# Stores of the first pair begun on GpSimd, and k times v with its weights' factors on VectorE, in a linear-attention block gated by a Hadamard feed-forward

## The chip, the cores and the metric

The kernel runs on one core of one Trainium2 chip. A core has TensorE (PE, matrix products, with weight loads listed as PEld), VectorE (DVE), ScalarE (ACT), GpSimd (POOL) and SyncE (SP), each with a queue of instructions that it takes in order, and DMA engines that move data between DRAM and the on-chip memory. The metric is the device time of one execution in microseconds (us), lower is better.

## The reference

The input x is 8 x 512 x 512 in fp32 (batch, length L, width D). Everything is computed in fp32.

```python
xn = layernorm(x)
# s: linear attention, 16 heads of 32
q, k, v = (xn @ W.T + b for each of Wq, Wk, Wv)
phi_q, phi_k = elu(q) + 1, elu(k) + 1
kv = cumsum(phi_k * v, axis=length)         # elementwise, no products between channels
s = ((phi_q * kv) * 32**-0.5) @ Wo.T + bo
# g: feed-forward, inner width 2048, Hadamard transforms (fwht) around the weights
h = fwht(xn * SU_ug)
u = silu((h @ W_gate.T) * scale_gate) * ((h @ W_up.T) * scale_up)
g = silu((fwht(u * SU_dp) @ W_down.T) * scale_dp)
return x + s * g
```

## The kernel before, in words

**Products in seven.** Every large matrix product is done in 2 x 2 blocks with seven products in place of eight (P1, P2, P7, P3, P4, P5, P6 are the seven places). For that, each weight and each set of tokens is first turned into seven factors: four blocks are loaded, and three more plus a new P7 are made by four additions (`encode_weights`, L305 to L308; `encode_tokens`, L297 to L300). On the gate and up weights this is done twice, one level inside the other, from the point where the second level exists ("gu" weights, L630).

**Pairs.** The batch is taken in 4 pairs p = 0..3 of two elements. A pair goes through: layernorm and transposes; attention in two groups g of channels (k, v, q in turn; then elu plus one, the product k times v, the cumulative sums along the length as scans, and q times the sums, `co`, with its factors); then 4 units u of the inner width. A unit makes the gate (`gate`, silu on ACT), the up part (`up`, gate times up is `ho`, with its factors), and after units 1 and 3 half of the down projection (`down`). `project_out` (output projection, `pz_o`, `px_o`) stands in unit 0.

**The first pair is different.** It reads the raw weights. For gate, up and down the Hadamard transform is put into the weights: butterflies on VectorE (L930 to L933 for gate and up, L969 and L974 for down), a product with a small Hadamard matrix on TensorE (`pw_gate`, `pwd`), a scale on ACT (L945, and in `fold_down`). The factors are made once and stored in DRAM for the later pairs, which only stream them: `keep_w` (L319) stores the factors of k, v, q, o; `inner_w` (L391 to L414) makes the outer factors of gate and up from the weights `w0` and `w1` in a three-slot tile `s_gate` or `s_up` (L408) and stores each factor as it is made (L400, into `d_gu`); `down_w` (L388) and `first_half_down` (L1018) store those of down (`d_down`), from `wd_f`, which `fold_down` (L997) stores. In `inner_w`, P5 goes to slot 0, P6 to slot 1, P3 to slot 2, and P7 to slot 0 again, so that P7 waits until the store of P5 has read its slot. All these stores, 73 in number, are begun on SP, which also begins nearly all loads. Units 0 to 2 of the first pair use `gate` and `up`; unit 3, and all units of later pairs, use `hidden_unit` with the streamed weights.

**What sets the order.** The program is traced in the order of an agenda: `at(place, fn)` puts a step so many places ahead, and `advance` runs through them; a group of seven products with two steps each is 14 places. Work for VectorE that is not urgent is put in the lists `later` (with `soon=True`: the urgent one) and handed out by `pace` behind each sum of an output (L468, the sum of a copied PSUM bank and another bank). `get_w` asks for weights three ahead, so that their loads, folds and factors (the `steps`) are spread over the groups before. `background` gives traced work a lower priority. A scheduler then fixes one queue per engine. Buffers come from pools (4 weight tiles, 6 tiles `t8` of 8 KB a partition, 6 snapshots, one `xin` tile for x or the s tiles, PSUM banks px 3, py 1, pz 2, t 2), so that a load can wait for the last reader of the tile that was there.

**What the change touches.** `keep_w`, `down_w`, `inner_w`, `fold_down`, `first_half_down` (the stores); `inner_w` (the last factor); `with_v` (L716, k times v on GpSimd, two operations of 128 x 1024) and `sums` (L722, four scans of 128 x 512 on VectorE); `up` (L793 to L798, ho and its factors on GpSimd, one of the products on VectorE); `first_w` (the factors of k, v, q and o on GpSimd). Other steps named later: L180, the layernorm scale of the first x; L271 to L284, the transposes and the tokens' factors `xo`; L333, factors of `wd` for the second half of down; L350 and L367, loads of raw gate weights and of `wd`; L528, products of o and down; L661, a sum of the two-level products; L777, silu of the gate; L831 and L835, sums of 128 x 1024 on GpSimd in `hidden_unit`.

Of the kernel before, what the change touches and what calls it, by code (L numbers as in the profile page):

```python
# [10 lines left out]
ALU = mybir.AluOpType  # L11
# [6 lines left out]
P1, P2, P7, P3, P4, P5, P6 = range(7)  # L18
# [3 lines left out]
def kernel(  # L22
# [27 lines left out]
    nc = tc.nc  # L50
    P = 128
    B, L, D = x.shape
# [5 lines left out]
    NU = NG // 2  # L58
# [27 lines left out]
    def later(us, fn, *args, soon=False):  # L86
        (urgent if soon else idle).append((us, fn, args))
# [16 lines left out]
    at = 0  # L104
# [13 lines left out]
    ones = const.tile([P, 1], F32, tag="ones", name="ones")  # L118
# [197 lines left out]

    def keep_w(name, w):
        d = dram.tile([P, 2 * 7 * P], F32, tag=f"d_{name}", name=f"d_{name}")
        nc.sync.dma_start(d, w.rearrange("p j s e -> p (j s e)"))  # L319
        kept[name] = d  # L320
        return w

# [51 lines left out]
    def down_w(u, j):  # L374

        t = t8.tile([P, 2, 7, P], F32, tag="t", name=f"wd_{u}_{j}")
        w = by_factor(t)
        rows_w(w, wd_f, u + NU * j, NG)

        def encode():  # L380
            for o, a, b, op in (
                (P5, P7, P4, ALU.add), (P6, P5, P1, ALU.subtract), (P3, P2, P6, ALU.subtract), (P7, P1, P7, ALU.subtract)
            ):
                later(0.5, nc.vector.tensor_tensor, w[:, o], w[:, a], w[:, b], op)
            later(0.0, store)

        def store():
            nc.sync.dma_start(wd[u // 2][:, :, 2 * (u % 2) + j], w)  # L388
            wd_made[u // 2] += 1

        at(8, encode)  # L391

    def inner_w(m, u, w0, w1):

        if u not in inner:
            inner[u] = dram.tile([P, 7, 2, 7, P], F32, tag=f"d_gu_{u}", name=f"d_gu_{u}")
        d = inner[u][:, :, ("gate", "up").index(m)]

        def store(c, t):
            nc.sync.dma_start(d[:, :, c, :], t)  # L400

        store(P1, w0[:, 0])
        store(P2, w0[:, 1])
        store(P4, w1[:, 1])
        t = xin.tile([P, 3, 7, P], F32, tag="x", name=f"s_{m}_{u}")

        def made(c, i, a, b, op):
            nc.vector.tensor_tensor(t[:, i], a, b, op)  # L408
            store(c, t[:, i])

        later(1.0, made, P5, 0, w1[:, 0], w1[:, 1], ALU.add, soon=True)
        later(1.0, made, P6, 1, t[:, 0], w0[:, 0], ALU.subtract, soon=True)
        later(1.0, made, P3, 2, w0[:, 1], t[:, 1], ALU.subtract, soon=True)
        later(1.0, made, P7, 0, w0[:, 0], w1[:, 0], ALU.subtract, soon=True)  # L414

# [4 lines left out]
    def at(place, fn):  # L422
        agenda.append((now[0] + place, now[1], fn))
        now[1] += 1
# [259 lines left out]
    def attention(p, xo, co, get_w):  # L684
        def project(m, g, then):
            w = get_w(m, g)
            r = t8.tile([P, 2, 2, L], F32, tag="t", name=f"{m}_{p}_{g}")
            b = (col("b" + m, g), col("b" + m, g + 2))

            def whole(px):  # L690
                nc.scalar.activation(r[:, 0, 1], px, AF.Identity, bias=b[0])  # L691
                then(r)

            group(
                f"{m}_{p}_{g}", [w[:, 0], w[:, 1]], x_rhs(xo),
                (r[:, 0, 0], r[:, 1, 0], r[:, 1, 1]), whole, b,
            )

        def elu_plus_one(r, name):
            neg = t8.tile([P, 2, 2, L], F32, tag="t", name=f"neg_{name}")  # L700
            for h in range(2):
                nc.scalar.activation(neg[:, h], r[:, h], AF.Relu, scale=-1.0)
                nc.scalar.activation(neg[:, h], neg[:, h], AF.Exp, scale=-1.0)
                nc.vector.scalar_tensor_tensor(r[:, h], r[:, h], 1.0, neg[:, h], ALU.add, ALU.max)

        def heads(g):
            phi = {}

            def with_k(k):
                phi["k"] = k  # L710
                elu_plus_one(k, f"k_{p}_{g}")

            def with_v(v):
                k = phi["k"]
                for h in range(2):
                    nc.gpsimd.tensor_tensor(v[:, h], v[:, h], k[:, h], ALU.mult)  # L716
                at(4, lambda: sums(k, v))

            def sums(k, v):
                for h in range(2):  # L720
                    for s in range(2):
                        nc.vector.tensor_tensor_scan(  # L722
                            k[:, h, s], ones.to_broadcast([P, L]), v[:, h, s], 0.0, ALU.mult, ALU.add
                        )

            def with_q(q):
                k = phi["k"]
                elu_plus_one(q, f"q_{p}_{g}")
                for h in range(2):
                    nc.vector.scalar_tensor_tensor(  # L730
                        co[:, g, h : h + 3 : 2, :], k[:, h], QSCALE, q[:, h], ALU.mult, ALU.mult
                    )
                encode_tokens(nc.gpsimd, co[:, g])

            project("k", g, with_k)
            project("v", g, with_v)
            project("q", g, with_q)

        for g in range(2):
            heads(g)  # L740
# [43 lines left out]
        )  # L784
        return g

    def up(p, f, g, xo, ho, get_w):

        w = get_w("up", f)
        r = t8.tile([P, 2, 2, L], F32, tag="t", name=f"u_{p}_{f}")  # L790

        def with_up(px):
            nc.gpsimd.tensor_tensor(ho[:, P1], g[:, 0, 0], r[:, 0, 0], ALU.mult)  # L793
            nc.vector.tensor_tensor(ho[:, P7], g[:, 0, 1], px, ALU.mult)
            nc.gpsimd.tensor_tensor(ho[:, P2 : P3 + 1 : 2], g[:, 1], r[:, 1], ALU.mult)
            encode_tokens(nc.gpsimd, ho)

        group(  # L798
            f"up_{p}_{f}", [w[:, 0], w[:, 1]], x_rhs(xo),
            (r[:, 0, 0], r[:, 1, 0], r[:, 1, 1]), with_up,  # L800
        )
# [181 lines left out]
    def fold_down(o):  # L983
        r = rs[:, o % 2]
        for a in range(NF // 4):
            p = ps.tile([P, 4, P], F32, tag="t", name=f"pwd_{o}_{a}")
            tc.keep_in_program_order(
                nc.tensor.matmul(
                    p.rearrange("p c e -> p (c e)"), had,
                    r[:, 4 * a : 4 * a + 4].rearrange("p c e -> p (c e)"), start=True, stop=True,  # L990
                )
            )
            for c in range(4):
                nc.scalar.activation(
                    r[:, 4 * a + c], p[:, c], AF.Copy, scale=su_dp[:, 4 * a + c : 4 * a + c + 1]
                )
        nc.sync.dma_start(wd_f[:, o * P : (o + 1) * P].rearrange("(c p) e -> p c e", p=P), r)  # L997

    def first_half_down():

        n = 4 * 2 * P
        w = [rd[:, i * n : (i + 1) * n] for i in range(7)]
        for a in range(2):
            for b in range(2):
                t = w[(P1, P2, P7, P4)[2 * a + b]].rearrange("p (u j e) -> u p j e", u=2, j=2)
                d = wd_f[:, a * 2 * P : (a + 1) * 2 * P].rearrange("(b j u p) e -> b u p j e", b=2, j=2, p=P)
                for u in range(2):
                    nc.sync.dma_start(t[u], d[b, u])

        def factors():  # L1010
            for i, x, y, op in (
                (P5, P7, P4, ALU.add), (P6, P5, P1, ALU.subtract), (P3, P2, P6, ALU.subtract), (P7, P1, P7, ALU.subtract)
            ):
                later(1.2, nc.vector.tensor_tensor, w[i], w[x], w[y], op, soon=True)
            later(0.0, at, 4, store, soon=True)

        def store():
            nc.sync.dma_start(wd[0].rearrange("p i k e -> p (i k e)"), rd)  # L1018
            wd_made[0] = 4

        at(8, factors)
# [4 lines left out]
    def first_w(m, g):  # L1026


        if m == "gate":
            return folded_w(m, wgate_t, g)  # L1030
        if m == "up":
            return folded_w(m, wup_t, g)
        name, eng = f"{m}_{g}", nc.gpsimd
        if m == "o":
            t = new_w(name)
            w = by_factor(t)
            rows_w(w, wo_t, g, 2)
        else:
            t = w = raw_w(name, sources[m], 0, 2, 1, g * P, 2 * P)

        def encode():
            encode_weights(eng, w)
            keep_w(name, t)

        return w, [(5, encode)]
# [131 lines left out]
    for p in range(B // 2):  # L1177
# [11 lines left out]
        for u in range(NU):  # L1189
            if p == 0 and u < NU - 1:  # L1190
# [3 lines left out]
                    project_out(p, co, get_w)  # L1194
                ho = hop.tile([P, 2, 7, L], F32, tag="h", name=f"ho_{p}_{u}")
                for m in range(2):
                    up(p, u + m * NU, gs[m], xo, ho[:, m], get_w)
            else:
                if p == 0:
                    catch_up()  # L1200
# [78 lines left out]
```

## Time and profile before

| | before |
|---|---|
| median of 3 runs | 1566.42 us (1566.15 to 1566.45) |
| the profiled execution | 1564.62 us |
| its span on the core | 1562.8 us (1.8 us lie around it) |
| mean granted TensorE clock | 0.993 |
| busy: PE, PEld, DVE, ACT, POOL | 98%, 72%, 63%, 27%, 32% |
| instructions: PE, DVE, ACT, POOL | 5924, 1379, 664, 280 |
| DMA queue q1 (hardware, from SP) | 272.27 MB, 53.3% of 16 engines |

The profile is one execution. A row of a group or a timeline names the line of the kernel, the engine, the operation and "out<-in" by the program's names. "idle before <-" tells how long an engine stood before the instruction and what it waited for. `pz_q`, `px_gate` and the like are PSUM banks, named for the bank and the stage. A matmul in fp32 of the program shows as two rows of the trace.

### The profile page before, as it was taken

To read this page: it belongs to the slowest core of one execution; us is meant where nothing else is said; L and a number is where in the kernel's file an instruction comes from. 1 tells how busy PE (TensorE), PEld (TensorE's weight loads), DVE (VectorE), ACT (ScalarE), POOL (GpSimd) and SP (SyncE) were. 2 spreads that over 40 slices of the span, in tenths; PEclk is the share of its full clock that TensorE was granted. 3 is DMA by queue.
4 is the path that set the end of the run, shared out by engine and by line. 5 is a ranking of instruction groups with operands and counts; after the bars stand their busy time and mean duration, and the time that the engine had idled before them with its cause. 6 is when DMAs were issued, how large, how long until landed. Compare 5 with 4: busy or idle time off the path is not lost.

```text
span 1562.8 us, 15732 instructions
## 1 busy us (share of the span) xinstructions
PE 1529.4 (98%) x5924; PEld 1127.0 (72%) x5924; DVE 985.1 (63%) x1379; ACT 418.8 (27%) x664; POOL 497.5 (32%) x280
## 2 busy tenths in 40 slices
PE   7999999998999999999999999999999999999998
PEld 3335545845884588888885488888886468888887
DVE  5897785677866674716676574725675476543673
ACT  4443341142114521112215431111212431111211
POOL 4633144004321262304612235301622236110731
PEclk9999999999999999999999999999999999999999
DMA  8244867797785344344575434336474233535462
GB/s 280 78 153 152 268 218 225 232 275 270 200 304 196 91 158 155 108 152 165 157 286 213 102 137 148 135 102 195 153 249 171 85 106 117 185 99 177 155 260 85
DMA packets 197693, 273.31 MB, mean 175 GB/s; under 512 B 56817, under 2 KB 155121, under 8 KB 193393
## 3 DMA queue, kind: packets, MB, share of 16 engines
q1 hardware_dynamic: 197472, 272.27, 53.3%
q8 instruction: 47, 0.77, 0.2%
q14 instruction: 30, 0.24, 0.0%
q10 hardware_dynamic: 144, 0.03, 0.0%
HBM read 196.25 MB, written 76.02 MB: 174 GB/s over the span
## 4 chain that ended last, share of the span: by engine, by line
PE 88%; DVE 4%; DMA 3%; issue 2%; POOL 1%; ACT 1%; SPq 1%; POOLq 0%; DVEq 0%; ACTq 0%
PE px_gu L630 20%; PE px_dn L528 13%; PE pz_gu L630 10%; PE pz_dn L528 6%; PE py_gu L630 5%; PE py_dn L528 4%; PE px_k L452 3%; PE px_v L452 3%; PE px_o L528 3%; PE px_q L452 3%; PE pz_o L528 2%; PE pz_k L452 2%; PE px_gate L452 2%; PE pz_q L452 2%; PE pz_v L452 1%
## 5 line engine op out<-in xcount | busy, mean ns | idle before, releaser
L630 PE MATMUL px_gu<-xo,w_gu 128*128 128x256 f32 x1456 | 348.9, 381 | 0.0
L630 PEld LDWEIGHTS px_gu<-xo,w_gu 128*128 128x128 f32 x1456 | 277.5, 191 | 44.2 <-issue 5.0
L528 PE MATMUL px_dn<-w_down,ho 128*128 128x256 f32 x1024 | 228.9, 379 | 0.0
L528 PEld LDWEIGHTS px_dn<-w_down,ho 128*128 128x128 f32 x1024 | 194.9, 190 | 28.7 <-issue 2.9
L630 PE MATMUL pz_gu<-xo,w_gu 128*128 128x256 f32 x728 | 188.6, 382 | 5.4 <-DVE a L661 5.2
L831 POOL TENSOR_TENSOR u<-u,v 128x1024 f32<-128x1024 f32 x26 | 60.8, 2363 | 371.2 <-DVE u L668 347.5
L630 PEld LDWEIGHTS pz_gu<-xo,w_gu 128*128 128x128 f32 x728 | 138.3, 191 | 26.2 <-DVE a L661 6.1
L528 PE MATMUL pz_dn<-w_down,ho 128*128 128x256 f32 x496 | 112.4, 380 | 3.2 <-DVE u L468 3.2
L528 PEld LDWEIGHTS pz_dn<-w_down,ho 128*128 128x128 f32 x496 | 93.9, 190 | 17.0 <-DVE u L468 3.6
L630 PE MATMUL py_gu<-xo,w_gu 128*128 128x256 f32 x364 | 93.5, 379 | 0.0
L876 POOL TENSOR_TENSOR s<-s,d 128x512 f32<-128x512 f32 x30 | 40.0, 1333 | 165.5 <-ACT d L875 126.4
L716 POOL TENSOR_TENSOR v<-v,k 128x1024 f32<-128x1024 f32 x16 | 43.0, 2685 | 138.9 <-ACT v L691 111.2
L630 PEld LDWEIGHTS py_gu<-xo,w_gu 128*128 128x128 f32 x364 | 69.3, 190 | 9.3
L835 POOL TENSOR_TENSOR v<-v,r 128x1024 f32<-128x1024 f32 x26 | 60.9, 2362 | 27.7 <-DVE r L668 27.7
L793 POOL TENSOR_TENSOR ho<-g,u 128x512 f32<-128x512 f32 x6 | 10.9, 1812 | 161.0 <-DVE u L468 151.1
L452 PE MATMUL px_k<-xo,w_k 128*128 128x512 f32 x128 | 61.6, 603 | 0.0
L452 PE MATMUL px_v<-xo,w_v 128*128 128x512 f32 x128 | 60.8, 595 | 0.0
L821 ACT ACTIVATE a<-a,cols_sb 128x512 f32<-128x512 f32 x26 | 18.8, 722 | 155.2 <-DVE a L668 153.4
L452 PE MATMUL px_q<-xo,w_q 128*128 128x512 f32 x128 | 60.2, 593 | 0.0
L722 DVE TENSOR_TENSOR_SCAN k<-ones,v 128x512 f32<-128x512 f32 x32 | 40.9, 1317 | 28.6 <-POOL v L716 28.6
L528 PE MATMUL px_o<-w_o,co 128*128 128x256 f32 x256 | 58.4, 380 | 0.0
L875 ACT ACTIVATE d<-d 128x512 f32<-128x512 f32 x31 | 19.5, 630 | 144.5 <-DVE d L543 102.4
(264 smaller groups left out, 2476.5 us busy)
## 6 DMA issues: line engine op xcount, KB each, us to landing
w_gu<-d_gu SPq DMA_DIRECT2D x91, 896.0 KB, 4.4
w_down<-d_down SPq DMA_DIRECT2D x56, 512.0 KB, 3.6
d_s<-o SPq DMA_DIRECT2D x8, 1024.0 KB, 4.3
d_d<-dn SPq DMA_DIRECT2D x8, 1024.0 KB, 7.7
d<-d_d SPq DMA_DIRECT2D x8, 1024.0 KB, 6.2
s<-d_s SPq DMA_DIRECT2D x8, 1024.0 KB, 8.1
y<-in_x_dram SPq DMA_DIRECT2D x8, 1024.0 KB, 7.3
out_dram<-y SPq DMA_DIRECT2D x15, 512.0 KB, 3.3
```

Source lines behind the costliest of these rows:

```text
L452: nc.tensor.matmul(p.rearrange("p a t -> p (a t)") if len(r.shape) == 2 else p, ws[k][:, i, :], r, start=(first and k == 0), stop=(k == n ...
L528: nc.tensor.matmul(p[:, c], t[:, (2 * g + c) * P : (2 * g + c + 1) * P], ws[i](k), start=(first and k == 0 and c == cs[0]), stop=(k == n - ...
L630: nc.tensor.matmul(p[:, lane], w[:, lane, i, :], x[:, i, :], start=(first and lane == 0), stop=True, skip_group_check=True,)
L716: nc.gpsimd.tensor_tensor(v[:, h], v[:, h], k[:, h], ALU.mult)
L722: nc.vector.tensor_tensor_scan(k[:, h, s], ones.to_broadcast([P, L]), v[:, h, s], 0.0, ALU.mult, ALU.add)
L793: nc.gpsimd.tensor_tensor(ho[:, P1], g[:, 0, 0], r[:, 0, 0], ALU.mult)
L821: nc.scalar.activation(g[:, m], g[:, m], AF.Silu, scale=col("w_gate", u + m * NU + a * NG))
L831: nc.gpsimd.tensor_tensor(r[:, m], ru1[:, m], rv[:, m], ALU.add)
L835: nc.gpsimd.tensor_tensor(rv[:, m], rv[:, m], rr[:, m], ALU.add)
L875: nc.scalar.activation(d, d, AF.Silu)
L876: (nc.vector if final and (a, s) == (1, 0) else nc.gpsimd).tensor_tensor(r, r, d, ALU.mult)
```

## The change

In words, part by part:

1. The 73 stores of the first pair's weights are begun by GpSimd (`nc.gpsimd.dma_start`) and not by SP. All loads, and the stores of x, s, d and out, stay on SP.
2. In `inner_w` the last factor, P7, is put on the list of urgent work 8 places later than before.
3. k times v is computed on VectorE, in all pairs. The scans come in two portions of two: the first 4 places after the products, the second 8 places after.
4. In `up`, the factors of ho are made on VectorE for the second up of an odd unit (in the first pair that is unit 1 alone, since unit 3 uses `hidden_unit`).
5. In `first_w`, the factors of the weights of k, v and q (6 weights, 4 operations of 128 x 256 each) are made on VectorE; those of o stay on GpSimd.

```diff
@@ keep_w
-        nc.sync.dma_start(d, w.rearrange("p j s e -> p (j s e)"))
+        nc.gpsimd.dma_start(d, w.rearrange("p j s e -> p (j s e)"))
@@ down_w, store
-            nc.sync.dma_start(wd[u // 2][:, :, 2 * (u % 2) + j], w)
+            nc.gpsimd.dma_start(wd[u // 2][:, :, 2 * (u % 2) + j], w)
@@ inner_w
         def store(c, t):
-            nc.sync.dma_start(d[:, :, c, :], t)
+            nc.gpsimd.dma_start(d[:, :, c, :], t)
...
-        later(1.0, made, P7, 0, w0[:, 0], w1[:, 0], ALU.subtract, soon=True)
+
+        def last():
+            later(1.0, made, P7, 0, w0[:, 0], w1[:, 0], ALU.subtract, soon=True)
+
+        later(0.0, at, 8, last, soon=True)
@@ attention, heads
             def with_v(v):
                 k = phi["k"]
                 for h in range(2):
-                    nc.gpsimd.tensor_tensor(v[:, h], v[:, h], k[:, h], ALU.mult)
-                at(4, lambda: sums(k, v))
-
-            def sums(k, v):
-                for h in range(2):
-                    for s in range(2):
-                        nc.vector.tensor_tensor_scan(
-                            k[:, h, s], ones.to_broadcast([P, L]), v[:, h, s], 0.0, ALU.mult, ALU.add
-                        )
+                    nc.vector.tensor_tensor(v[:, h], v[:, h], k[:, h], ALU.mult)
+                    at(4 + 4 * h, lambda h=h: sums(k, v, h))
+
+            def sums(k, v, h):
+                for s in range(2):
+                    nc.vector.tensor_tensor_scan(
+                        k[:, h, s], ones.to_broadcast([P, L]), v[:, h, s], 0.0, ALU.mult, ALU.add
+                    )
@@ up
-    def up(p, f, g, xo, ho, get_w):
+    def up(p, f, g, xo, ho, get_w, last):
...
-            encode_tokens(nc.gpsimd, ho)
+            encode_tokens(nc.vector if last else nc.gpsimd, ho)
@@ fold_down
-        nc.sync.dma_start(wd_f[:, o * P : (o + 1) * P].rearrange("(c p) e -> p c e", p=P), r)
+        nc.gpsimd.dma_start(wd_f[:, o * P : (o + 1) * P].rearrange("(c p) e -> p c e", p=P), r)
@@ first_half_down, store
-            nc.sync.dma_start(wd[0].rearrange("p i k e -> p (i k e)"), rd)
+            nc.gpsimd.dma_start(wd[0].rearrange("p i k e -> p (i k e)"), rd)
@@ first_w
-        name, eng = f"{m}_{g}", nc.gpsimd
+        name, eng = f"{m}_{g}", nc.gpsimd if m == "o" else nc.vector
@@ the units of the first pair
-                    up(p, u + m * NU, gs[m], xo, ho[:, m], get_w)
+                    up(p, u + m * NU, gs[m], xo, ho[:, m], get_w, u % 2 == 1 and m == 1)
```

## The prediction

> **What bounds the kernel now.** I read the page first: which engine fills the span, and where it does not.
>
> ```profile
> PE 1529.4 (98%) x5924; PEld 1127.0 (72%) x5924; DVE 985.1 (63%) x1379; ACT 418.8 (27%) x664; POOL 497.5 (32%) x280
> ...
> PE   7999999998999999999999999999999999999998
> ...
> DVE  5897785677866674716676574725675476543673
> ...
> PE 88%; DVE 4%; DMA 3%; issue 2%; POOL 1%; ACT 1%; SPq 1%; POOLq 0%; DVEq 0%; ACTq 0%
> ```
>
> TensorE is the bound: 98% busy, 88% of the chain that ended last. No part of the change takes a matmul away, so only TensorE's holes can be won. The waits of TensorE list them all:
>
> ```profile
> PE pt L271 <- ACT x L178: 7.4, 1, 7.4
> PE pz_gu L630 <- DVE a L661: 5.2, 1, 5.2
> PE pz_q L452 <- DVE q L468: 3.4, 1, 3.4
> PE pz_dn L528 <- DVE u L468: 3.2, 1, 3.2
> PE pwd L988 <- ACT w_gate L945: 3.2, 1, 3.2
> PE pz_o L528 <- DVE g L468: 2.9, 1, 2.9
> PE px_gate L452 <- ACT sc_gate L462: 0.9, 1, 0.9
> ```
>
> The 7.4 is the start, which waits for x. Of the other six, four end on VectorE; of the two on ACT the larger, w_gate, stood behind a Silu that waited for VectorE's g. The busy time by stretch says when:
>
> ```profile
> 40.00:80.00 40.00, 36.59 (x83) 15.68 (x82) 35.28 (x30) 16.78 (x32) 23.66 (x14) 0.96 0.26 84
> 80.00:120.00 40.00, 36.85 (x79) 15.67 (x78) 39.38 (x42) 21.29 (x40) 16.63 (x8) 0.91 0.44 138
> ...
> 400.00:800.00 400.00, 400.00 (x1683) 319.10 (x1682) 244.37 (x343) 96.87 (x136) 128.67 (x62) 1.00 0.55 178
> ```
>
> (Columns: length, then busy time of PE, PEld, DVE, ACT, POOL, granted clock, DMA share, GB/s.) From 400 us on TensorE has no hole. Before, VectorE is nearly full (39.38 of 40) and the clock falls where TensorE has idled: in TensorE's timeline the 4 to 6 matmuls after a hole start 0.85 us apart instead of 0.43. So I count a hole as the excess of each matmul's start-to-start time over the median of its shape: 2.1 us in 0-40, 5.4 in 40-80, 6.6 in 80-120, 6.1 in 120-160, 3.5 in 240-280, 8.9 in 360-400, about 1 in all the rest: 33.8. That is the most the change can win beyond the start.
>
> What made VectorE late at 106 us:
>
> ```profile
> 96.51 6.14 POOL L716 TENSOR_TENSOR v<-v,k 128x1024 f32<-128x1024 f32 x1 [5.97 <-DVE v L468]
> ```
> ```profile
> 100.44 0.66 DVE L468 TENSOR_TENSOR q<-sc_q,pz_q 128x512 f32<-128x512 f32 x1
> 101.02 5.93 DVE L722 TENSOR_TENSOR_SCAN k<-ones,v 128x512 f32<-128x512 f32 x3
> 106.86 0.66 DVE L468 TENSOR_TENSOR g<-sa_gate,py_gate 128x512 f32<-128x512 f32 x1
> ```
>
> The product k times v took 6.14 us on GpSimd (2.36 where undisturbed, as L831's), the scans wait for it and lie in VectorE's queue ahead of the sum g that TensorE's next work needs. And at 132 us:
>
> ```profile
> 132.33 1.09 DVE L408 TENSOR_TENSOR s_gate<-w_gate,w_gate 128x896 f32<-128x896 f32 x1 [7.15 <-DMA d_gu<-s_gate]
> ```
>
> VectorE stands still for 7.15 us: factor P7 overwrites slot 0 of the s tile, whose store was begun on SP only at 125.1, behind d_o (issued 124.19, it waited for GpSimd's w_o) and wd_f.
>
> **The change, part by part.**
>
> *k times v on VectorE, scans halved.* In the first pair 4 products leave GpSimd (2.34, 3.26, 2.72, 6.14) and cost VectorE 4 x 1.21 = 4.8 us (L969, also 128x1024 with two inputs, is 1.21 undisturbed). Gone: 3.61 us idle before the scan at 48.06 (VectorE's timeline), and most of the inflation of VectorE's two-input operations beside GpSimd's (L969 1.21 to 3.37, scans 1.21 to 2.7), 11.8 us summed over 42-107. GpSimd keeps the w_o and co factors there, so I credit 8 of 11.8. In the new instruction order q's sum sc_q stands ahead of group 0's scans, so **hole 1 (5.4)** loses its cause. In group 1 the scans still stand ahead of g's sum. Against 4.8 stand also 8 weight factors (w_v, w_q of group 1) that now fall in 60-75 us: 8 x 0.36 (four of L305-308 take 1.45 on VectorE) = 2.9. VectorE in 42-107: +7.7 - 3.6 - 8 = 3.9 us earlier, against a wait of 3.2: of **hole 2 (6.6)** I take 5.0. The 12 products of the later pairs (14.5 us) fall where TensorE never waits and VectorE is 60% busy: 0; without that cover up to 14.5.
>
> *Factors of k, v, q.* 16 of the 24 instructions land in 13-28 us, 5.8 us of VectorE work, against 0.81 + 0.35 + 4.84 us of idle time there, but three come ahead of a layernorm scale that the last transposes wait for. Loss between 0 and 3 us; I take 1, as most of the idle is near them.
>
> *P7 of the inner factors, 8 places later.* The agenda counts places; a group has 14, with 28 matmuls in the trace of 0.43 us = 12 us, so 8 places are 6.9 us. VectorE no longer stands for 7.15 at 125-132: **holes 3 and 4 (6.1)**, taken whole. Next late there is P7's own store, which the second pair's streamed weights want only after 400 us.
>
> *73 stores from SP to GpSimd* (8 kept, 4 factors of down, 56 of gate and up, 4 wd_f, 1 d_down). Moved past SP's queue, they no longer hold the loads behind them. **Hole 5 (3.5):** the w_gate loads issued at 250-255 behind s_up stores landed as late as 259.97, VectorE idled 5.34, then u's sum came at 265.63. I take 2.5. **Hole 6 (8.9):** the load of wd was issued at 374.04 behind d_down stores that waited for VectorE, landed at 379.48, and VectorE idled 4.57 with `a` behind it; I take 4.5, since that load also needs a buffer which GpSimd frees after other stores.
>
> The price of a store begun by GpSimd is nowhere in this trace: no DMA is issued there. From below SP's rows give 0.33-0.52 us an issue; from above I take GpSimd's slowest row, 6.14. I take 1.0: the nearest row is SP's issue of the same transfer (0.52), and GpSimd takes about twice VectorE's time for the same operation (2.36 against 1.21). What waits behind a store is the gated product ho and its factors, and co's: in 238-262 us four s_gate and three s_up stores stand ahead of the ho factors of unit 1, whose last ended at 257.26, 0.6 us before the matmuls pz_dn began (257.82). 3 stores not hidden x 1.0 less 0.6: about 2.4 us, and the like at 362-382. I take 3 us for all new waits of this kind, between 0 and 12.
>
> By the Trainium skill ("DMA: Bandwidth & Descriptors", section "Issuing engines are not separate DMA queues") starting DMAs from several engines saves only the small issue time, and its section "Issuing engine by pattern" sends simple stores to SyncE. By that rule the stores' part would be worth 0, or a loss: 73 issues x 0.5 us leave an SP that bounds nothing. The rows at 125 and 374 speak otherwise: what is saved is not issue but the standing behind a waiting store. No run shows yet which holds.
>
> The ho factors on VectorE (`last`, the second up of unit 1 only) is 4 x 0.68 = 2.7 us where VectorE idles 4 to 5; taken as 0.
>
> **Sum.** 5.4 + 5.0 + 6.1 + 2.5 + 4.5 - 1 - 3 = 19.5 us. From the profiled execution's 1564.6 (span 1562.8, 1.8 around it): 1545.1. The median of the timed runs is 1.8 above that execution, so **1547**. Bounds of this case: all holes and no new wait, 31 less; only holes 1 to 4 with 3 of loss at the start and 3 of waits (10.5): so 12 to 28, 1538 to 1554.
>
> **Rivals.**
>
> *VectorE stays the bound of the first 125 us.* It is 39.38 of 40 busy there and gets 7.7 us more; if the inflation comes from VectorE's own pairing with GpSimd's co and w_o factors, or from DMA, and not from k times v, it is late by 7.7 - 3.6 = 4.1 more at g's sum: hole 2 becomes 10.7, hole 1 goes, holes 5 and 6 half: 5.4 - 4.1 + 6.1 + 6.2 - 4 (start and new waits) = 9.6 us, 1557; with hole 6 whole or untouched, 4 to 12: 1554 to 1563. For it: VectorE's load. Against: the products' neighbours are the inflated rows.
>
> *GpSimd's queue chokes (slower).* In 120-280 us it is busy 51.4 us (windows), of which about 6 go; some 33 stores come into these 160 us. At c us each it needs 45 + 33c: it fills from c = 3.5, and at 4.2 its lateness, handed to ho and then to pz_dn, eats the 22 us won elsewhere. At 5 it is 50 late: 1566.4 - 22 + 50 = 1594; at 4.5 (34 late) 1578. For it: disturbed rows of 6.14 exist and a store here has 896 pieces of 512 bytes. Against: 128x512 undisturbed is only 1.26.
>
> *No change.* The holes return elsewhere because each store only changes the engine whose queue it blocks: the loads wait for buffers that GpSimd frees. 1563.3 to 1569.5.
>
> **How the numbers follow.** Forecast 0.55, VectorE 0.20, no change 0.06, choke 0.19. 0.2% of 1566.4 is 3.1 us, about what a measurement of this kernel tells from no change: faster 0.75, same 0.06, slower 0.19. The range reaches from 1536, two below the forecast's own end since hole 6 may go whole, up to 1566, through the VectorE case and half of no change; the choke stays outside. The likeliest case's own range is 1538 to 1554.
>
> **What would show it.** Right: the waits of TensorE without pz_q <- q, pwd <- w_gate and pz_o <- g; VectorE without the 7.15 before L408 and 3.61 before L722; a matmul excess of 10 to 20 us before 400. The stores: a new DMA queue, POOL's issues 0.5 to 2 us each. Wrong: TensorE waiting for co or ho on POOL (choke), for g's sum at 105-115 (VectorE stays the bound), a first matmul of px_k over 2 us later (start), or a hole after 400 us.

## The result and the profile after

The changed kernel takes 1589.06 us (median, 1586.49 to 1590.34) against 1566.43 us before (1566.15 to 1568.37): ratio 1.0137, 95% interval 1.0124 to 1.0150, some 21 us slower. 1547 was forecast. The profiled execution, the slowest of the four (1590.34 us), has a span of 1588.5 us against 1562.8, 25.7 longer. One execution of `no_defer`, a run told below, took 4190 us and counts in no ratio; it is the profiled one, so the holes of that run can't be read.

The page after, its rows of busy time, slices and DMA queues:

```profile
PE 1534.0 (97%) x5924; PEld 1127.0 (71%) x5924; DVE 1011.1 (64%) x1423; ACT 418.0 (26%) x664; POOL 497.8 (31%) x309
...
PE   7988979998899999999999999999999999999998
...
POOL 1352255226322125301622126210632117110731
...
q1 hardware_dynamic: 133200, 227.70, 43.8%
q0 software_dynamic: 10512, 44.57, 7.3%
```

The matmuls are the same 5924. GpSimd is not full anywhere in the first quarter (no slice above 6 tenths). There is one new queue, q0, which carries the 73 stores: its 44.57 MB are what q1 has lost (272.27 MB before). TensorE's slices fall to 7 and 8 where they were 9 before, and the waits of TensorE say on what:

```profile
PE pw_up L942 <- DVE r_up L936: 7.3, 1, 7.3
PE pt L271 <- ACT x L178: 7.3, 1, 7.3
PE pwd L991 <- ACT rd L997: 6.3, 1, 6.3
PE pz_gu L634 <- DVE u L472: 6.0, 2, 4.3
PE pz_o L532 <- DVE g L472: 4.2, 1, 4.2
PE pz_gu L634 <- DVE a L676: 3.6, 1, 3.6
PE px_gate L456 <- ACT sb_gate L466: 3.2, 1, 3.2
PE py_gu L634 <- DVE a L653: 2.5, 1, 2.5
PE pw_gate L942 <- DVE r_gate L936: 2.3, 1, 2.3
PE pz_dn L532 <- POOL ho L300: 2.1, 1, 2.1
```

(Lines after the edit in `inner_w` are 3 to 4 higher than before: L468 is L472, L528 is L532.) `pz_q <- q` has gone. `pwd` and `pz_o`, whose waits the prediction had gone too, now wait 6.3 us (for another line) and 4.2, and the list has become longer. Counted as in the prediction, as the excess of each matmul's start-to-start time over the median of its shape, in us by stretch of the span:

| stretch | before | after | only VectorE | only stores | only late P7 | VectorE + late P7 | VectorE + 4 stores |
|---|---|---|---|---|---|---|---|
| 0-40 | 2.1 | 1.5 | 2.6 | 2.3 | 1.8 | 2.3 | 1.8 |
| 40-80 | 5.4 | 0.6 | 0.5 | 4.5 | 5.4 | 0.5 | 0.5 |
| 80-120 | 6.6 | 8.5 | 9.1 | 6.7 | 8.0 | 9.0 | 8.7 |
| 120-160 | 6.1 | 7.2 | 0.6 | 9.8 | 1.8 | 0.6 | 0.6 |
| 200-240 | 0.1 | 14.4 | 0.1 | 2.1 | 1.7 | 1.8 | 0.1 |
| 240-360 | 3.5 | 8.6 | 5.1 | 7.3 | 5.8 | 3.2 | 4.9 |
| 360-400 | 8.9 | 9.2 | 8.8 | 9.2 | 6.7 | 7.5 | 6.9 |
| 400-480 | 0.2 | 8.4 | 0.7 | 0.2 | 12.9 | 15.1 | 0.5 |

(The other columns are experiments told below: `only_vector`, `only_stores`, `only_defer`, `after_sp`, `vector_4`.) From before to after these rows grow by 25.5 us, which is nearly all of the lengthening of the span (25.7). The largest is 200-240. VectorE's timeline of the kernel after shows it:

```profile
205.07 2.15 DVE L408 TENSOR_TENSOR s_up<-w_up,w_up 128x896 f32<-128x896 f32 x1
207.14 0.67 DVE L472 TENSOR_TENSOR g<-sa_gate,py_gate 128x512 f32<-128x512 f32 x1
207.74 0.68 DVE L797 TENSOR_TENSOR ho<-g,px_up 128x512 f32<-128x512 f32 x1
222.03 0.69 DVE L933 TENSOR_TENSOR r_up<-w_up 128x512 f32<-128x512 f32 x1 [13.62 <-DMA w_up<-in_wup_t_dram]
```

VectorE makes the late P7 of s_up at 205.07 to 207.22, and then stands 13.62 us for a raw load of w_up. SP's queue and GpSimd's timeline of the same kernel:

```profile
207.28 7.03 SPq L350 DMA_DIRECT2D w_up<-in_wup_t_dram  x8
```
```profile
206.23 2.11 POOL L299 TENSOR_TENSOR ho<-ho 128x512 f32<-128x512 f32 x1
208.29 0.57 POOL L1021 DMA_DIRECT2D d_down<-rd  x1
208.86 0.97 POOL L400 DMA_DIRECT2D d_gu<-s_up  x1
```

And SP's queue of the kernel before:

```profile
194.34 1.95 SPq L350 DMA_DIRECT2D w_up<-in_wup_t_dram  x4
196.45 0.37 SPq L129 DMA_DIRECT2D x<-in_x_dram  x1
196.92 1.23 SPq L400 DMA_DIRECT2D d_gu<-w_gate  x2
206.31 0.34 SPq L1018 DMA_DIRECT2D d_down<-rd  x1
```

Before, P7 was made at 192.02, the load began at 194.34 and had landed by 198.5, long before the 3584 KB store at 206.31. After, the load begins 0.06 us after P7 ends: P7 is the last to read the two weight tiles, and the load needs the buffer of one of them. The store begins 1 us later on the other queue (its data were ready at 205.14, but it stood 3.2 us behind ho's factors in GpSimd's queue); of the eight loads the first three land in 2.1 to 2.7 us, the other five, begun from 208.73 on, at 221.81 to 223.30, after the store, which landed at 219.73. Before, four more loads of w_up, begun on SP from 208.07 on, landed behind the same store too (217.85 to 219.01), but the stretch has only 0.1 us of holes: what costs is that the first four are late as well.

### The profile page after: what moved, and what is told of

It is laid out like the page before. It is cut to its first block, busy times and chain, and to the rows that moved or that the text cites. A ratio compares the mean times of both kernels' runs of the same rounds, so it can differ in the third digit from the quotient of the medians.

```text
span 1588.5 us, 15808 instructions
## 1 busy us (share of the span) xinstructions
PE 1534.0 (97%) x5924; PEld 1127.0 (71%) x5924; DVE 1011.1 (64%) x1423; ACT 418.0 (26%) x664; POOL 497.8 (31%) x309
## 3 DMA queue, kind: packets, MB, share of 16 engines
q0 software_dynamic: 10512, 44.57, 7.3%
## 4 chain that ended last, share of the span: by engine, by line
PE 76%; DVE 1%; DMA 1%; POOL 0%; issue 0%; ACT 0%; POOLq 0%; SPq 0%; DVEq 0%; ACTq 0%
PE px_gu L634 20%; PE px_dn L532 12%; PE pz_gu L634 10%; PE pz_dn L532 6%; PE py_gu L634 5%; PE py_dn L532 3%; PE px_v L456 3%; PE px_o L532 3%; PE px_k L456 3%; PE px_q L456 3%; PE pz_o L532 1%; PE pz_k L456 1%; PE pz_q L456 1%; PE pz_v L456 1%; PE px_gate L456 1%; PE px_up L456 1%
## 5 line engine op out<-in xcount | busy, mean ns | idle before, releaser
L532 PE MATMUL px_dn<-w_down,ho 128*128 128x256 f32 x1024 | 228.8, 379 | 0.0
L532 PEld LDWEIGHTS px_dn<-w_down,ho 128*128 128x128 f32 x1024 | 194.6, 190 | 29.0 <-issue 2.9
L532 PE MATMUL pz_dn<-w_down,ho 128*128 128x256 f32 x496 | 113.6, 382 | 3.8 <-POOL ho L300 2.1
L532 PEld LDWEIGHTS pz_dn<-w_down,ho 128*128 128x128 f32 x496 | 94.2, 191 | 18.2 <-POOL ho L300 2.5
L297 POOL TENSOR_TENSOR co<-co 128x512 f32<-128x512 f32 x8 | 14.0, 1747 | 208.4 <-DVE co L733 205.3
L532 PE MATMUL px_o<-w_o,co 128*128 128x256 f32 x256 | 58.4, 379 | 0.0
L532 PE MATMUL py_dn<-w_down,ho 128*128 128x256 f32 x256 | 57.9, 379 | 0.0
L824 ACT ACTIVATE u<-u,cols_sb 128x512 f32<-128x512 f32 x52 | 36.9, 720 | 78.2 <-DVE u L672 75.0
```

Of the source, the lines that this page charges most:

```text
L297: eng.tensor_tensor(o[..., P5, :], o[..., P7, :], o[..., P1, :], ALU.subtract)
L532: nc.tensor.matmul(p[:, c], t[:, (2 * g + c) * P : (2 * g + c + 1) * P], ws[i](k), start=(first and k == 0 and c == cs[0]), stop=(k == n - ...
L824: nc.scalar.activation(g[:, m], g[:, m], AF.Silu, scale=col("w_gate", u + m * NU + a * NG))
```

## The experiments

Three theories. **A**: the late P7 holds two weight buffers and the one s tile longer, so that the next loads start later. **B**: the stores now stand in the queue of GpSimd, behind its co and ho work, and delay what their landing sets free (and the ho and co work behind them). **C**: VectorE is overloaded. Ratios are to the kernel before on the same chip, with their 95% interval.

| run | what of the change it has | median us | ratio (interval) |
|---|---|---|---|
| after | all | 1589.06 | 1.0137 (1.0124 to 1.0150) |
| no_defer | all but the late P7 | 1567.32 | 1.0007 (0.9997 to 1.0017) |
| only_defer | late P7 | 1576.46 | 1.0055 (1.0041 to 1.0069) |
| only_stores | 73 stores on GpSimd | 1573.93 | 1.0042 (1.0029 to 1.0054) |
| only_vector | parts 3 to 5, on VectorE | 1560.07 | 0.9957 (0.9945 to 0.9970) |
| after_sp | VectorE part and late P7 | 1569.58 | 1.0016 (1.0005 to 1.0027) |
| big_store_sp | all, d_down<-rd on SP | 1582.42 | 1.0106 (1.0093 to 1.0119) |
| vector_17 | VectorE part, 17 stores on GpSimd | 1559.91 | 0.9964 (0.9952 to 0.9976) |
| vector_56 | VectorE part, 56 stores on GpSimd | 1566.32 | 0.9997 (0.9988 to 1.0006) |
| p7_sp | as vector_56, 8 stores of P7 on SP | 1562.65 | 0.9969 (0.9958 to 0.9981) |
| p5_sp | as vector_56, 8 stores of P5 on SP | 1564.99 | 0.9986 (0.9974 to 0.9999) |
| vector_act | VectorE part, 73 stores on ScalarE | 1576.38 | 1.0071 (1.0058 to 1.0083) |
| vector_defer4 | VectorE part, P7 4 places late | 1565.49 | 0.9993 (0.9982 to 1.0004) |
| kv_only | k times v and scans only | 1560.31 | 0.9951 (0.9939 to 0.9963) |
| vector_4 | VectorE part, 4 stores on GpSimd | 1556.96 | 0.9928 (0.9915 to 0.9942) |
| vector_4_g1 | the same, second group's factors back | 1556.80 | 0.9933 (0.9915 to 0.9952) |

### The parts one by one

`no_defer` is the changed kernel with (the `def last` around the old line goes too)

```diff
-        later(0.0, at, 8, last, soon=True)
+        later(1.0, made, P7, 0, w0[:, 0], w1[:, 0], ALU.subtract, soon=True)
```

> The changed kernel with P7 made at once, as before; all else changed. Theory A (the late P7 keeps two weight buffers and the one s tile, so the next loads start about 13 us later and meet the big d_down store): the 14.4 us of holes in 200-240 go, and part of those at 138 and 271; 1563 to 1572. Theory B (stores in GpSimd's queue hold ho, co and the loads back): no more than 4 us better than the changed kernel, 1585 or above. Theory C (VectorE overloaded): as B in 80-120, little else, 1580 or above.

Measured 1.0007: the late P7 costs 20 us in this company (0.0130 of 1566). Theory A, by the time; whether the 14.4 us of 200-240 went, no trace shows.

`only_defer` is the kernel before with the edit of `inner_w` that makes P7 late, and nothing else.

> The kernel before with the late P7 alone. Theory A: slower than before by 8 to 25 us, with holes in 200-280 before the folds pw_up and pw_gate and w_up's raw loads begun right after the late P7. Theories B and C: faster, by the 6.1 us of holes 3 and 4 as predicted, 1558 to 1563.

Measured 1.0055, 8.6 us slower; theory A, but not where I looked first: 200-280 has 3.4 us of holes, as many as before the edit (3.6). Holes 3 and 4 do shrink (6.1 to 1.8), as predicted, and the price is paid later. The waits of TensorE in this run:

```profile
PE py_dn L532 <- DVE d L547: 6.0, 1, 6.0
PE pz_gu L634 <- DVE u L472: 3.9, 1, 3.9
PE pz_q L456 <- DVE q L472: 3.4, 1, 3.4
```

The 6.0 lies at 436 us, where before there is no hole. It comes back with the same line in `after_sp`, where it is read below.

`only_stores` is the kernel before with `nc.gpsimd.dma_start` in the five places of the 73 stores.

> The kernel before with the 73 stores begun by GpSimd alone; k times v and the factors of k, v, q stay on GpSimd behind them. Theory A: between 1556 and 1570. Theory B: 1575 or above, with holes that end on GpSimd's co or ho, or on loads that wait for GpSimd. Theory C: at or a little below 1566.

Measured 1.0042, 6.6 us slower: between the two forecasts in time, but with the holes of theory B. GpSimd's timeline of this run, and the one row of VectorE that answers to the 132.33 of before:

```profile
119.72 2.17 POOL L297 TENSOR_TENSOR co<-co 128x512 f32<-128x512 f32 x1 [0.30 <-DVE co L730]
121.97 2.00 POOL L298 TENSOR_TENSOR co<-co 128x512 f32<-128x512 f32 x1
123.93 2.11 POOL L300 TENSOR_TENSOR co<-co 128x512 f32<-128x512 f32 x1
126.01 2.12 POOL L299 TENSOR_TENSOR co<-co 128x512 f32<-128x512 f32 x1
128.06 1.21 POOL L997 DMA_DIRECT2D wd_f<-rd  x1
129.27 2.90 POOL L400 DMA_DIRECT2D d_gu<-s_gate  x3
```
```profile
135.29 1.09 DVE L408 TENSOR_TENSOR s_gate<-w_gate,w_gate 128x896 f32<-128x896 f32 x1 [7.21 <-DMA d_gu<-s_gate]
```

P5 of s_gate is ready at 122.84 (its row begins at 121.29 and takes 1.55). Its store, which must read slot 0 before P7 may be written, begins at 129.27, behind co's four factors and wd_f; on SP it had begun at 125.11. VectorE stands 7.21 us where it stood 7.15: the wait has only changed its queue, and it ends 3 us later.

`only_vector` is the changed kernel with the stores on SP and P7 at once.

> The kernel before with k times v, the two portions of scans, the factors of k, v, q and the second ho of unit 1 on VectorE; stores on SyncE, P7 at once. Theories A and B: hole 1 (5.4 us) gone and hole 2 about as before, 1558 to 1564. Theory C: 1568 or above, with VectorE full in 40-120 and the holes after it larger.

Measured 0.9957, 6.7 us faster. Hole 1 is gone (5.4 to 0.5), and holes 3 and 4 too (6.1 to 0.6), which I had put down to the late P7 and the stores: with k times v off GpSimd the factors of w_o are ready sooner, so the store d_o (begun at 117.74, before at 124.19) no longer holds SP's queue. Theory C falls.

`kv_only` leaves the factors of k, v, q and ho on GpSimd as before.

> The kernel before with k times v on VectorE and the scans in two portions alone; all factors as before on GpSimd. If hole 1 (5.4 us) goes by the product leaving GpSimd: 1559 to 1562. If the factors of k, v, q are what frees GpSimd: hole 1 stays in part, 1563 to 1566.

Measured 0.9951: in time k times v alone brings it all, and the factors bring nothing that can be measured. The forecast's other sign came half true: of the 5.4 us in 40-80, 2.9 stay. They are another wait, though: `pz_q <- q` is gone, and `px_k` waits 2.6 us for ScalarE's sc_k at 66. In `only_vector` this wait is 0.2, but `pwd` waits 6.3 in place of 5.0.

### The late P7

`after_sp` is the changed kernel with all stores on `nc.sync`.

> The changed kernel with all 73 stores back on SyncE; the late P7 and the work moved to VectorE stay. Theory A (the late P7 holds weight buffers and the s tile): its 10 us alone come on top of the 1560 of the VectorE part, 1567 to 1573, with loads of w_up and w_gate begun right after each late P7. Rival D (the late P7 is harmful only together with stores on GpSimd): 1562 or less.

Measured 1.0016 against 0.9957 of `only_vector`: 9 us for the late P7 alone, theory A. SP's queue in `only_vector` and then in `after_sp`:

```profile
187.21 1.95 SPq L350 DMA_DIRECT2D w_up<-in_wup_t_dram  x4
```
```profile
196.43 0.34 SPq L1021 DMA_DIRECT2D d_down<-rd  x1
198.50 0.51 SPq L400 DMA_DIRECT2D d_gu<-s_up  x1
199.10 10.05 SPq L350 DMA_DIRECT2D w_up<-in_wup_t_dram  x8
```

P7 of s_up comes at 184.90 in the first and at 196.32 in the second, and with it the loads begin 12 us later, now behind the big store. VectorE in `after_sp`, at the hole of 430 us:

```profile
432.58 0.69 DVE L543 TENSOR_TENSOR sa_dn<-px_dn,d 128x512 f32<-128x512 f32 x1 [9.45 <-DMA d<-d_d]
```

The load of d stands on SP (issued 425.39) behind eight loads of z, which wait for the store of the next pair's x, issued at 408.16 and not at 392.50 as in `only_vector`. The load of that x was begun at 379.02 and not at 370.31. x uses the same single buffer as the s tiles, and the last P7 came at 364.29 in place of 354.57, but the buffer is not what this load waited for: P7's store had landed at 369.37. The load of x stood in SP's queue behind a load of w_gu, which waited 6.9 us for TensorE:

```profile
378.60 0.33 SPq L327 DMA_DIRECT2D w_gu<-d_gu  x1
379.02 0.39 SPq L129 DMA_DIRECT2D x<-in_x_dram  x1
```

`only_defer` has the same order, with its hole at 436; in `before` and `only_vector` x's load follows wd's loads, and there is no such hole. So a P7 that comes 10 us later at 364 comes back as a hole of 6.7 us at 430, by x's place in SP's queue; that the late P7 sets this place is likely from these runs, but not shown.

`vector_defer4` has 4 places in place of 8.

> The VectorE part alone, with P7 made 4 places late and not 8; stores on SyncE. Theory A (the cost is the time for which the late P7 holds buffers): between the 1560 of no delay and the 1570 of 8 places, 1562 to 1567. Rival D (no cost from the delay itself): 1560 or less.

Measured 0.9993, between 0.9957 and 1.0016, as theory A has it; it is no clean half dose, since P7 of s_up came at 195.42, only 0.9 us sooner than with 8 places. x's load stands behind wd's loads again (377.90), and the 6.7 us at 430 are gone; 1.9 us are left there, of another wait (for w_down). Most of its cost lies in 240-360: 9.4 us of holes, against 5.1 in `only_vector`.

`big_store_sp`:

```diff
-            nc.gpsimd.dma_start(wd[0].rearrange("p i k e -> p (i k e)"), rd)
+            nc.sync.dma_start(wd[0].rearrange("p i k e -> p (i k e)"), rd)
```

> The changed kernel with only the 3584 KB store d_down<-rd back on SyncE, where it stands behind the raw loads of w_up in the same queue. If the 14.4 us of holes in 200-240 come from that store being begun by GpSimd 1 us after the late loads started and the rest of these loads lying behind it on the DMA engines: those loads land within 5 us of their issue and the time falls by 7 to 13 us, 1576 to 1582. If the lateness of the loads alone makes the hole (buffer held by the late P7): at most 4 us better.

Measured 1.0106 against 1.0137: about 5 us better, less than I expected, and for another reason than mine. On SP the store went ahead of the loads (202.91, loads from 204.99), and all eight landed between 216.22 and 220.03, about 11 us after the first was begun. The fourth load, for which VectorE waits, landed at 217.39 in place of 221.81, and the stretch fell from 14.4 to 7.8. So late loads meet that store in both, and the queue that begins the store decides how late they land. In `after_sp` they meet it too, but there the store began at 196.43 and had landed at 206.46, and 1.8 us of holes are left.

### The stores

`vector_17` begins the kept factors, wd_f and d_down on GpSimd and leaves gate and up on SP; `vector_56` does the opposite. Both have the VectorE part and P7 at once.

> The VectorE part alone, with 17 of the 73 stores (kept factors, wd_f, d_down) begun by GpSimd and the 56 of gate and up on SyncE; P7 at once. Theory B (a store is delayed by GpSimd's ho and co work ahead of it and delays them): the 56 with their slot to be freed cost most, so 1558 to 1563 here, near the 1560 without them. Rival E (each transfer begun by GpSimd is dearer for itself, landing later): cost goes with the bytes, and 17 stores are 15 of 40 MB, so 1562 to 1565.

> The VectorE part with only the 56 stores of gate and up begun by GpSimd, the other 17 on SyncE; P7 at once. Theory B (a store that frees a slot of the s tile stands behind co's and ho's work in GpSimd's queue, so VectorE's next factor waits longer): 1564 to 1570, with s stores begun several us after their factor and VectorE standing before P7 of s_gate or s_up. Rival F (no single set of stores costs, only all 73 together do): 1558 to 1562.

Measured 0.9964 and 0.9997 beside the 0.9957 without: the 56 cost 6 us, the 17 together nothing that can be measured. (The 17 carry 18.9 of the 44.6 MB, not 15 of 40, which doesn't change what the run says of rival E.) But the 17 are no even lot: four of them, `vector_4` below, win 4.5 us, so the other 13 lose 5.6 (0.9964 against 0.9928). In the trace of `vector_17` the stretch 360-400 falls to 5.1, while `pwd` waits 8.2 us for 6.3 and 200-240 has 6.2; why was not taken apart. In `vector_56` VectorE's idle time ahead of the factors at L408 is 11.9 us in sum, 4.8 in `only_vector`. One part lies at 126 us as in `only_stores`, behind co (2.4 us). The largest wait of VectorE is this, in GpSimd's timeline, SP's queue and VectorE's timeline of `vector_56`:

```profile
238.73 0.90 POOL L400 DMA_DIRECT2D d_gu<-s_gate  x1 [1.50 <-DVE s_gate L408]
```
```profile
238.56 0.84 SPq L335 DMA_DIRECT2D w_down<-d_down  x2
239.45 2.55 SPq L350 DMA_DIRECT2D w_gate<-in_wgate_t_dram  x4
```
```profile
245.81 1.09 DVE L408 TENSOR_TENSOR s_up<-w_up 128x896 f32<-128x896 f32 x1 [4.99 <-DMA d_gu<-s_gate]
```

The store of the last factor of s_gate is begun 0.3 us after the factor ends, so it stands behind nothing. But SP begins six loads in the same 3.5 us, and the store lands 7.0 us after its issue; the s tile of s_up needs its buffer, so VectorE waits 4.99. In `only_vector` the store and the loads are in one queue, the store first, and only two of the six loads come within 4 us of it: it lands in 3.4 us, and the same wait is 0.72. I call this theory G: on a queue of its own the store loses its precedence over loads. Two more runs take one of the two causes away each. `p7_sp` is `vector_56` with the P7 stores on SP, `p5_sp` with those of P5:

```diff
-            nc.gpsimd.dma_start(d[:, :, c, :], t)
+            (nc.sync if c == P7 else nc.gpsimd).dma_start(d[:, :, c, :], t)
```

> As vector_56, but the 8 stores of P7 (the last of each s tile) on SyncE, ahead of the loads traced after them. Theory G (a store on its own queue loses its precedence over loads that SyncE begins at the same moment, lands 3 us later, and the next s tile waits for it): the P7 store of s_gate at 238 lands within 4 us and 2 to 5 of the 6 us come back, 1561 to 1564. Theory B in its narrow form (only the standing behind co and ho counts): no change, 1565 to 1567.

> As vector_56, but the 8 stores of P5 (whose slot P7 needs) on SyncE. Theory B in its narrow form: the wait before P7 of s_gate at 126 goes, and with it most of the 3.7 us of holes in 120-160, 1562 to 1564. Theory G: no more than 1 us better, 1565 to 1567.

Measured 0.9969 and 0.9986: some 4.4 and 1.7 of the 6.3 us come back. VectorE's row in `p7_sp`:

```profile
241.84 1.09 DVE L408 TENSOR_TENSOR s_up<-w_up 128x896 f32<-128x896 f32 x1 [2.51 <-DMA d_gu<-s_gate]
```

The store lands 4.7 us after issue with the same six loads behind it, not 7.0, and the wait is halved (within 4 us was forecast). In `p5_sp` the wait before P7 at 126 is gone and the stretch 120-160 falls from 4.3 to 0.5, as theory B said, though 80-120 grows from 8.5 to 11.2. So both mechanisms are there in the traces. Which is the larger is not shown. The 4.4 us are clear of the intervals, the 1.7 are not. And a wait of VectorE is not a hole of TensorE: in 240-360, where theory G's row lies, the holes are 5.1 us in `only_vector`, 6.9 in `vector_56` and 5.7 in `p7_sp`, so of the 4.4 this row explains about 1.2.

`vector_act` begins all 73 stores by `nc.scalar.dma_start`.

> The VectorE part alone, with all 73 stores begun by ScalarE (a hardware queue as SyncE's); P7 at once. Theory B (what costs is that stores wait in the queue of an engine with work of its own): slower than 1560, by more than GpSimd's 7 us since ScalarE's copies of PSUM stand behind the waiting stores, 1570 to 1590. Rival E (the software descriptors of GpSimd are the cost): 1556 to 1562.

Measured 1.0071, 18 us slower than `only_vector`: a hardware queue doesn't help, if the engine has work of its own that stands behind the waiting store. TensorE there waits for ScalarE's copies (sc_up 4.8, sc_gate 3.2). Theory B.

`vector_4` begins only the four stores `d_down<-wd` (L388) on GpSimd.

> The VectorE part with only the 4 stores d_down<-wd begun by GpSimd. If the loads of wd behind these stores make the hole at 372 (8.8 us with its tail): about 4 to 6 us of it go, 1554 to 1557. If the load waits for its buffer anyway: 1559 to 1561.

Measured 0.9928 (0.9915 to 0.9942), the lowest ratio of all, faster than both kernels. SP's queue of `only_vector`, and then of `vector_4`:

```profile
364.75 0.52 SPq L388 DMA_DIRECT2D d_down<-wd  x1
365.36 1.75 SPq L367 DMA_DIRECT2D wd<-wd_f  x2
367.21 0.53 SPq L388 DMA_DIRECT2D d_down<-wd  x1
367.78 2.19 SPq L367 DMA_DIRECT2D wd<-wd_f  x2
```
```profile
358.82 1.75 SPq L367 DMA_DIRECT2D wd<-wd_f  x4
```

The loads no longer stand behind two stores that wait for VectorE and begin 6.5 us sooner; VectorE's wait of 4.46 ahead of L333 is gone, and `pz_gu` waits 2.9 in place of 5.2. The stretch 360-400 falls by 1.9 us, less than the time does: the rest of the 4.5 was not found in one place.

`vector_4_g1` has, beside that,

```diff
-        name, eng = f"{m}_{g}", nc.gpsimd if m == "o" else nc.vector
+        name, eng = f"{m}_{g}", nc.vector if g == 0 and m != "o" else nc.gpsimd
```

> As vector_4, with the factors of v, q, k of the second group back on GpSimd, which takes 8 operations (2.9 us) off VectorE at 60-66. If VectorE's load makes the hole of 9 us at 106: 2 to 4 us better than vector_4. If GpSimd's operations slow VectorE's as much: equal to it or worse.

Measured the same as `vector_4` (0.9933): without these 2.9 us on VectorE `pwd` waits 5.4 in place of 6.3 us, the stretch 80-120 stays (8.6 for 8.7), and `px_k` waits 2.6 us at 66 as in `kv_only`.

## Why the prediction was wrong, point by point

**The bound, and k times v: right.** Only TensorE's holes could be won. Hole 1 went whole as forecast (5.4 to 0.6), and the VectorE products of the later pairs cost nothing (440 to 800 us: TensorE busy 360.00 of 360.00; from 480 us to the end 2.0 us of holes, 1.9 before).

**Hole 2: the working was right, the next thing late was not seen.** g's sum was to come 3.9 us earlier; it came at 102.39 and not 106.86, 4.5 earlier. But another wait took the place of the one removed. VectorE and ScalarE after:

```profile
102.39 0.66 DVE L472 TENSOR_TENSOR g<-sa_gate,py_gate 128x512 f32<-128x512 f32 x1
102.97 2.35 DVE L977 TENSOR_TENSOR rd<-rd 128x1024 f32<-128x1024 f32 x2
...
107.50 0.68 DVE L472 TENSOR_TENSOR q<-sb_q,pz_q 128x512 f32<-128x512 f32 x1
```
```profile
108.22 1.06 ACT L706 ACTIVATE neg_q<-q 128x1024 f32<-128x1024 f32 x1 [4.41 <-DVE q L472]
109.18 0.35 ACT L997 ACTIVATE rd<-pwd,su_dp 128x128 f32<-128x128 f32 x1
```

`pwd` now waits 6.3 us for ScalarE's scale of rd, which stands in ScalarE's queue behind neg_q, which waits for q's sum at 107.50. I credited 5.0 of 6.6; it became 8.5. The VectorE rival had hole 2 grow too (to 10.7), but by a late sum of g, which is not what happened.

**Holes 3 and 4: the failing step.** "Next late there is P7's own store, which the second pair's streamed weights want only after 400 us." VectorE indeed no longer stands at P7 (129.83, no idle time). What I left out is that P7 reads two weight tiles and keeps the s tile: what needs these buffers comes only after it. Nor was there anything left to win: in `only_vector`, with P7 at once, holes 3 and 4 are 0.6 us already, since k times v on VectorE had freed SP's queue. And 8 places are no fixed time: I took 6.9 us, but from `only_vector` to `after_sp` the eight P7 move by 0.9 to 17.6 us. The price appears in three places of the changed kernel. At 200-240 it is the 14.4 us read above. At 130 the raw load of w_up begins at 130.98, 0.07 us after P7 ends, VectorE stands 3.74 us for it at 139.26 and `pz_o` waits 4.2; this one needs the stores on GpSimd as well, for in `after_sp` the load begins at 131.98, lands in 2.6 to 3.1 us in place of 5.1 to 7.1, and 120-160 has 0.6 us. The third is the tile that x shares. The last P7 ends at 393.76 (before: 361.10), its store lands at 399.87, the load of x begins 0.12 us later, and VectorE stands 7.05 us for it. Behind it in VectorE's queue is the sum `a`, for which `pz_gu` waits 3.6 us:

```profile
408.40 1.29 DVE L140 BATCH_NORM_STATS2 st<-x 128x6 f32<-128x512 f32 x2 [7.05 <-DMA x<-in_x_dram]
```

`only_defer` and `after_sp` price the late P7 at 9 us, `no_defer` at 20 beside the stores. I had costed it at 6.1 of gain.

**The stores: price right, effect wrong; the other failing step.** An issue on GpSimd takes 0.53 to 1.4 us (d_gu 0.95 in the median), as I took it (1.0), and GpSimd is busy at most 25 us in each 40 us stretch of the first 440, so the choke that was my slower rival did not come: 2.1 us of TensorE's waits end on GpSimd's ho. That 1589 lies in the choke's 1578 to 1594 is chance. I asked what stands behind a store and priced that (3 us). I did not ask what the store itself stands behind, though the prediction's own row for hole 3 was a store that began late in a shared queue (in `only_stores` co's work, 4.2 us later than on SP), nor over what loads it had precedence on SP (7.0 us to landing for 3.4). Credited 2.5 + 4.5 for holes 5 and 6: only the four stores of `vector_4` bring such a gain (4.5 us); the other 13 of `vector_17` take 5.6 and the 56 take 6. That makes a loss of some 7 us, and `no_defer` against `only_vector` measures 7.8.

On the rule "Issuing engines are not separate DMA queues" (the Trainium skill, "DMA: Bandwidth & Descriptors"), which I set aside for the rows and by which the part would be worth 0 or a loss: it holds for 69 of the 73 stores, which lost. It misses the four that stood ahead of loads in SP's queue and waited for VectorE, where another queue was worth 4.5 us.

**The start: no loss.** 1 us was charged; the stretch 0-40 has 1.5 after and 2.1 before.

**The sum.** Right by run: VectorE part -6.7, where the terms for holes 1, 2 and the start said -9.4. Wrong sign: late P7 +9 (said -6.1) and stores +6.6 alone (said -4.0 with the new waits). Alone they add to 8.5 us; all together cost 21.5. Within the intervals the stores cost beside the VectorE part what they cost alone (`no_defer` 1.0007; the changes of the two ratios add to 0.9999), and so does the late P7 (`after_sp` 1.0016; added 1.0012). So the other 13 us come when the late P7 and the stores on GpSimd are together, two terms that my sum added as if neither touched the other; the two of them without the VectorE part were not run. Read from the traces are loads that the late P7 brings together with a big store (200-240) or with its own store (130), and the load of x behind the last store (400). Their shares of the 13 us are not shown.

## What to carry to other kernels

When work is put off to spare a wait, list the buffers that it reads and writes, who takes each next, and what load that taker begins: the tile held longer is the price, and with the loads that move back behind it, it may show 60 us later. Measure how far a step in places moves in time; it was 0.9 to 17.6 us here. When a DMA is moved to another queue, ask both what stands behind it and what it will stand behind; a queue of an engine with work of its own is a good place only for a store whose landing nobody waits for. One queue also sets an order among transfers (in these traces the transfers of a queue landed in the order in which they were begun): off it, a store whose landing frees a buffer competes with the loads that stood behind it. Move the few stores that a trace shows ahead of late loads, not all of a kind.

## What the runs showed of the hardware

- A 448 KB store of 896 rows takes GpSimd 0.95 us to begin (median in `after`; 0.90 in `vector_56`, single ones up to 1.4), SP 0.52; a 3584 KB store of whole rows only 0.57. From issue to landing the s_gate stores take 4.2 us (median) from GpSimd in `after`, 3.5 from SP before; the one of `vector_56` beside which SP begins six loads takes 7.0.
- A 3584 KB store lands 10.0 to 11.7 us after issue. 128 KB loads begun just after it land only behind it: 10 to 13 us after issue from another queue (`after`), 7.8 to 9.8 from the same one (`before`); those begun just before it land in 2.1 to 2.7.
- GpSimd's 128x256 sums of w_o took up to 4.26 us (`after`, at 91.74) beside VectorE's operations of two inputs, and 0.72 at best before.
